# Rebuilding the main loop of a pairwise outer-product kernel with batch normalisation: larger tiles, two buffers, W in PSUM, products shared with GpSimd, and a fixed order

## The chip, the cores and the metric

The kernel runs on one core of a Trainium2 chip. The metric is the device time of one execution in microseconds (us). The engines are named as the profile names them: PE is TensorE, DVE VectorE, ACT ScalarE, POOL GpSimd, SP SyncE, which here only issues DMAs.

## The reference, cut to what matters

```python
# r_xi, r_xj: (1024, 39, 16) float32; W: (1, 16, 16); gamma, beta: (741,)
rows, cols = np.tril_indices(39, k=-1)                  # 741 pairs (r, c) with c < r
cross = xj[:, rows, :, None] * xi[:, cols, None, :]     # (1024, 741, 16, 16)
mean = jnp.mean(cross, axis=(0, 2, 3), keepdims=True)   # one mean and variance for each pair
var = jnp.mean(jnp.square(cross - mean), axis=(0, 2, 3), keepdims=True)
normed = (cross - mean) * jax.lax.rsqrt(var + 1e-5)
normed = normed * gamma[None, :, None, None] + beta[None, :, None, None]
out = normed[:, :, None, :, :] * W[None, None, :, :, :]  # stored as (1024, 1, 741, 16, 16)
```

The output has 1024 x 741 x 256 numbers of 4 bytes, 777 MB. It is nearly all that moves: the inputs have 6 MB.

## The kernel before

The 1024 samples lie on the 128 partitions, eight samples on each. A first part, the head, works out for each pair a scale `s` and a shift `t` (tiles `s_sb` and `t_sb`), so that an output is (xj[b, r, i] x xi[b, c, j] x s[r, c] + t[r, c]) x W[i, j]. The head ends with the instructions of lines 149 to 151, and it stays as it is.

Then comes the main loop. It goes over the rows r = 1 to 38, short and long ones in turn (1, 38, 2, 37, ...). Row r has r pairs, c = 0 to r - 1. A tile is one row of `nt` samples on each partition, with `nt` the largest of 1, 2, 4 and 8 for which nt x r is below 39; so rows 20 to 38 have one sample in a tile, rows 10 to 19 two, rows 5 to 9 four. Each tile takes four steps:

- GpSimd multiplies the row's r vectors of `xi` by their scales into `xs` (line 166). There are two buffers of `xs`.
- ScalarE makes the products with `xj`: for each sample and each i of 16 one instruction over r x 16 elements, with xj[b, r, i] as its scale (line 183), into the tile `y`. For rows up to 6 VectorE makes them instead, one instruction a sample (line 175). There are four buffers of `y`.
- VectorE does the last step in place: one `scalar_tensor_tensor` for each pair c over nt x 256 elements, (y + t) x W (line 191), with `y` and W both in SBUF.
- SyncE issues one DMA that stores the tile (line 199).

The scheduler of the tile framework orders the instructions on each engine, and an instruction waits on semaphores for what it reads and for the buffer that it writes.

Of the kernel before, what the change touches and what calls it, by code (L numbers as in the profile page):

```python
# [7 lines left out]
F32 = mybir.dt.float32  # L8
AF = mybir.ActivationFunctionType
ALU = mybir.AluOpType  # L10
AX = mybir.AxisListType

BN_EPS = 1e-5
# Rows of at most this many pairs have their outer products on VectorE, the longer ones on ScalarE.
VECTOR_ROW = 6


@with_exitstack
def tile_pair_outer_batchnorm(
# [18 lines left out]
    nc = tc.nc  # L38
    P = nc.NUM_PARTITIONS
    NB, F, E = xi.shape  # L40
    NT = NB // P
    EE = E * E
# [14 lines left out]
    out_v = out.rearrange("(p t) o n i j -> p t (o n i j)", t=NT)  # L57
# [6 lines left out]
    with tc.tile_pool(name="stat", bufs=1) as st, tc.tile_pool(  # L64
        name="dev", bufs=2
# [6 lines left out]
        ones = st.tile([P, P], F32, name="ones")  # L72
        nc.gpsimd.memset(ones, 1.0 / NB)
# [16 lines left out]
        ma, mb, va, vb = (x[:, :, :, 0] for x in (ma, mb, va, vb))  # L90
# [6 lines left out]
        def pairs(engine, rows, cols, name):  # L97
            q = st.tile([P, NT, NP], F32, name=name)
            for r in range(1, F):
                engine.tensor_tensor(  # L100
                    q[:, :, first[r] : first[r] + r],
                    rows[:, :, r : r + 1].to_broadcast([P, NT, r]),
                    cols[:, :, 0:r],
                    ALU.mult,
                )
            return q
# [20 lines left out]
        mean = st.tile([P, 1, NP], F32, name="mean")  # L127
# [4 lines left out]
            nc.scalar.activation(q_a[:, t], q_a[:, t], AF.Square)  # L132
        batch_mean(ps_v, [q_a], False, True)

        # rstd = 1 / sqrt(var + eps), with a Newton step behind the table's square root
        var = st.tile([P, NP], F32, name="var")
        for acc, (n0, n1) in zip(ps_v, halves):
            nc.vector.tensor_scalar_add(var[:, n0:n1], acc[:, : n1 - n0], BN_EPS)  # L138
# [2 lines left out]
        rstd = st.tile([P, NP], F32, name="rstd")  # L141
# [12 lines left out]
    order = []  # L154
    for k in range(1, (F - 1) // 2 + 1):
        order += [k, F - k]
    assert sorted(order) == list(range(1, F))

    rows = ctx.enter_context(tc.tile_pool(name="rows", bufs=4))
    scaled = ctx.enter_context(tc.tile_pool(name="scaled", bufs=2))  # L160
    for r in order:
        n0 = first[r]
        nt = max(n for n in (1, 2, 4, 8) if NT % n == 0 and (n == 1 or n * r < F))
        for t0 in range(0, NT, nt):
            xs = scaled.tile([P, nt, r, E], F32, tag="xs", name=f"xs_{r}_{t0}")
            nc.gpsimd.tensor_tensor(  # L166
                xs,
                xi_sb[:, t0 : t0 + nt, 0:r, :],
                s_sb[:, :, n0 : n0 + r, :].to_broadcast([P, nt, r, E]),
                ALU.mult,  # L170
            )
            y = rows.tile([P, nt, r, E, E], F32, tag="y", name=f"y_{r}_{t0}")
            for t in range(nt):
                if r <= VECTOR_ROW:
                    nc.vector.tensor_tensor(  # L175
                        y[:, t],
                        xs[:, t].unsqueeze(2).to_broadcast([P, r, E, E]),
                        xj_sb[:, t0 + t, r : r + 1, :].unsqueeze(3).to_broadcast([P, r, E, E]),
                        ALU.mult,
                    )  # L180
                else:
                    for i in range(E):
                        nc.scalar.activation(  # L183
                            y[:, t, :, i, :],
                            xs[:, t],
                            AF.Copy,
                            scale=xj_sb[:, t0 + t, r, i : i + 1],
                        )
            y2 = y.rearrange("p t n i j -> p t n (i j)")
            for c in range(r):  # L190
                nc.vector.scalar_tensor_tensor(  # L191
                    y2[:, :, c, :],
                    y2[:, :, c, :],
                    t_sb[:, n0 + c : n0 + c + 1],
                    w_sb.to_broadcast([P, nt, EE]),
                    ALU.add,
                    ALU.mult,
                )
            nc.sync.dma_start(
                out_v[:, t0 : t0 + nt, n0 * EE : (n0 + r) * EE],  # L200
                y.rearrange("p t n i j -> p t (n i j)"),
            )


# [26 lines left out]
```

## Time and profile before

| | before |
|---|---|
| median of 3 runs | 3103.07 us (3102.97 to 3104.05) |
| span of the profiled execution (first to last instruction) | 3100.0 us |
| outside the span, by the median | 3.07 us |
| VectorE busy | 2448.0 us (79%) |
| ScalarE busy | 2015.7 us (65%) |
| GpSimd busy | 1659.1 us (54%) |
| written to HBM | 776.99 MB |
| DMA queue of SyncE, share of 16 engines | 59.1% |

The profiled execution has no time of its own beside its span; its 3100.0 us and the median differ by 3.07 us, a tenth of a per cent, which lie before the first and behind the last instruction.

How to read the lines of the profile. A group of instructions is shown as line, engine, operation, `out<-in`, shapes (partitions x elements of one partition), `x` count, then busy us and mean ns of one, then idle us of the engine ahead of them and who ended most of it. "Busy" counts overlapping instructions once, so busy divided by count is the distance from one start to the next where a stream has no holes, and the mean, which holds the filling and draining of the pipeline too, is longer. A row of the waits has who waited for whom, the total, the number of times, the longest. A row of the chain or of the order of time has start, duration and instruction. A row of the DMA issues has the size and the median time from issue to landing.

### The profile page before, as it was taken

The page shows a single profiled execution, that of the slowest core. Times are in us where ns is not written, and L with a number is a line of the kernel's source. Part 1 is how long each engine was busy: PE and PEld are TensorE (multiplying, and loading weights), DVE is VectorE, ACT ScalarE, POOL GpSimd, SP SyncE. Part 2 cuts the span into 40 slices and gives each one's busy share as a digit, 9 for nine tenths or more (in the row PEclk, how much of TensorE's full clock was granted, in tenths as well). Part 3 has the DMA queues.
Part 4 walks back from the last instruction along what each step waited for, and adds up shares of the span by engine and source line. Part 5 has one row for each costly group of instructions (what it writes and reads, how often), then busy time and mean ns, then how long its engine had stood idle before and what let it go on. Part 6 is the DMA issues. An engine that isn't in the chain of part 4 may idle for free.

```text
span 3100.0 us, 10969 instructions
## 1 busy us (share of the span) xinstructions
PE 45.6 (1%) x128; PEld 26.7 (1%) x128; DVE 2448.0 (79%) x5253; ACT 2015.7 (65%) x4117; POOL 1659.1 (54%) x252
## 2 busy tenths in 40 slices
PE   2300000000000000000000000000000000000000
PEld 1100000000000000000000000000000000000000
DVE  8687888888888787777777787768777777778786
ACT  2446455464635777777676767676868686868685
POOL 2375757665666656555646464646363636362623
PEclk9655555555555555555555555555555555555555
DMA  2165656566555656666656656565656565666666
GB/s 78 78 265 228 282 244 259 250 269 271 250 252 248 293 237 281 256 268 268 288 249 263 265 240 272 246 281 242 270 243 281 244 281 249 276 263 268 275 267 275
DMA packets 43653, 783.71 MB, mean 253 GB/s; under 512 B 3472, under 2 KB 4496, under 8 KB 11824
## 3 DMA queue, kind: packets, MB, share of 16 engines
q1 hardware_dynamic: 42784, 779.56, 59.1%
q10 hardware_dynamic: 576, 2.56, 0.2%
q0 software_dynamic: 208, 0.89, 0.1%
q14 instruction: 84, 0.69, 0.1%
q8 instruction: 1, 0.02, 0.0%
HBM read 6.00 MB, written 776.99 MB: 253 GB/s over the span
## 4 chain that ended last, share of the span: by engine, by line
ACT 48%; POOL 45%; DVE 3%; issue 2%; PE 1%; DMA 0%; POOLq 0%; DVEq 0%; ACTq 0%
ACT y L183 48%; POOL xs L166 45%; PE ps_v L111 1%; DVE y L191 1%; DVE q_a L100 1%; DVE dev L86 0%; PE ps_m L111 0%; DMA xj_sb<-in_r_xj_dram 0%; DVE ma L83 0%; DVE vb L88 0%; DVE va L88 0%; DVE mb L83 0%; DVE inv L140 0%; DVE rstd L146 0%; DVE inv L144 0%
## 5 line engine op out<-in xcount | busy, mean ns | idle before, releaser
L191 DVE SCALAR_TENSOR_TENSOR y<-y,t_sb,w_sb 128x256 f32<-128x256 f32 (+2 forms) x5068 | 2314.6, 534 | 610.3 <-ACT y L183 610.1
L183 ACT ACTIVATE y<-xs,xj_sb 128x608 f32<-128x608 f32 (+31 forms) x4096 | 1994.9, 580 | 978.7 <-POOL xs L166 978.7
L166 POOL TENSOR_TENSOR xs<-xi_sb,s_sb 128x576 f32<-128x576 f32 (+19 forms) x206 | 1637.3, 7958 | 1368.8 <-ACT y L183 1315.6
L175 DVE TENSOR_TENSOR y<-xs,xj_sb 128x256 f32<-128x256 f32 (+5 forms) x48 | 51.5, 1136 | 1.5 <-POOL xs L166 1.4
L100 POOL TENSOR_TENSOR q_c<-va,sb 128x8 f32<-128x8 f32 (+37 forms) x38 | 19.6, 553 | 39.3 <-DVE sb L93 39.3
L87 ACT ACTIVATE dev<-dev 128x1248 f32<-128x1248 f32 x8 | 9.9, 1243 | 26.1 <-DVE dev L86 25.9
L129 ACT COPY mean<-ps_m 128x371 f32<-128x371 f32 (+1 forms) x2 | 0.9, 468 | 31.0 <-PE ps_m L111 31.0
L138 DVE TENSOR_SCALAR var<-ps_v 128x371 f32<-128x371 f32 (+1 forms) x2 | 1.1, 545 | 22.1 <-PE ps_v L111 22.0
L100 DVE TENSOR_TENSOR q_a<-ma,mb 128x8 f32<-128x8 f32 (+37 forms) x38 | 18.2, 554 | 0.0
L142 ACT ACTIVATE rstd<-inv 128x741 f32<-128x741 f32 x1 | 0.8, 822 | 25.9 <-DVE inv L140 25.9
L111 PE MATMUL ps_m<-q_a,ones 128*128 128x371 f32 (+1 forms) x32 | 15.7, 662 | 56.1 <-DVE q_a L100 56.1
L83 DVE TENSOR_REDUCE ma<-xj_sb 128x78 f32<-128x1248 f32 x4 | 5.8, 1452 | 6.9 <-DMA xj_sb<-in_r_xj_dram 6.9
L111 PE MATMUL ps_v<-q_a,ones 128*128 128x371 f32 (+1 forms) x32 | 10.2, 474 | 0.0
L111 PE MATMUL ps_v<-q_b,ones 128*128 128x371 f32 (+1 forms) x32 | 10.2, 474 | 0.0
L111 PE MATMUL ps_v<-q_c,ones 128*128 128x371 f32 (+1 forms) x32 | 10.1, 474 | 0.0
L100 DVE TENSOR_TENSOR q_b<-sa,vb 128x8 f32<-128x8 f32 (+37 forms) x38 | 9.9, 341 | 0.0
L111 PEld LDWEIGHTS ps_m<-q_a,ones 128*128 128x128 f32 x32 | 8.5, 274 | 62.7 <-issue 57.0
L131 DVE TENSOR_TENSOR q_a<-q_a,mean 128x741 f32<-128x741 f32 x8 | 6.8, 925 | 1.6 <-ACT mean L129 1.6
L132 ACT ACTIVATE q_a<-q_a 128x741 f32<-128x741 f32 x8 | 6.6, 822 | 1.1 <-DVE q_a L131 1.0
L111 PEld LDWEIGHTS ps_v<-q_a,ones 128*128 128x128 f32 x32 | 6.1, 189 | 3.9
L111 PEld LDWEIGHTS ps_v<-q_c,ones 128*128 128x128 f32 x32 | 6.1, 189 | 3.9
L111 PEld LDWEIGHTS ps_v<-q_b,ones 128*128 128x128 f32 x32 | 6.1, 189 | 3.9
(30 smaller groups left out, 49.6 us busy)
## 6 DMA issues: line engine op xcount, KB each, us to landing
out_dram<-y SPq DMA_DIRECT2D x14, 4608.0 KB, 12.4
out_dram<-y SPq DMA_DIRECT2D x15, 4096.0 KB, 11.2
out_dram<-y SPq DMA_DIRECT2D x12, 4864.0 KB, 12.9
out_dram<-y SPq DMA_DIRECT2D x12, 4352.0 KB, 11.8
out_dram<-y SPq DMA_DIRECT2D x14, 3584.0 KB, 10.0
out_dram<-y SPq DMA_DIRECT2D x15, 3072.0 KB, 8.8
out_dram<-y SPq DMA_DIRECT2D x12, 3840.0 KB, 10.6
out_dram<-y SPq DMA_DIRECT2D x12, 3328.0 KB, 9.3
```

The source lines that it names most:

```text
L83: nc.vector.tensor_reduce(ms[:, :, :, 0], xs, AX.X, ALU.add)
L87: nc.scalar.activation(dev, dev, AF.Square)
L100: engine.tensor_tensor(q[:, :, first[r] : first[r] + r], rows[:, :, r : r + 1].to_broadcast([P, NT, r]), cols[:, :, 0:r], ALU.mult,)
L111: nc.tensor.matmul(acc[:, : n1 - n0], ones, q[:, t, n0:n1], start=start and k == 0, stop=stop and k == len(qs) * NT - 1,)
L129: nc.scalar.copy(mean[:, 0, n0:n1], acc[:, : n1 - n0])
L131: nc.vector.tensor_sub(q_a[:, t], q_a[:, t], mean[:, 0])
L132: nc.scalar.activation(q_a[:, t], q_a[:, t], AF.Square)
L138: nc.vector.tensor_scalar_add(var[:, n0:n1], acc[:, : n1 - n0], BN_EPS)
L166: nc.gpsimd.tensor_tensor(xs, xi_sb[:, t0 : t0 + nt, 0:r, :], s_sb[:, :, n0 : n0 + r, :].to_broadcast([P, nt, r, E]), ALU.mult,)
L175: nc.vector.tensor_tensor(y[:, t], xs[:, t].unsqueeze(2).to_broadcast([P, r, E, E]), xj_sb[:, t0 + t, r : r + 1, :].unsqueeze(3).to_broadc ...
L183: nc.scalar.activation(y[:, t, :, i, :], xs[:, t], AF.Copy, scale=xj_sb[:, t0 + t, r, i : i + 1],)
L191: nc.vector.scalar_tensor_tensor(y2[:, :, c, :], y2[:, :, c, :], t_sb[:, n0 + c : n0 + c + 1], w_sb.to_broadcast([P, nt, EE]), ALU.add, AL ...
```

## The change

The main loop is written anew; the head is untouched.

- W is copied once into PSUM by ScalarE (`w_dve`, line 160). VectorE's last step reads it there. GpSimd reads W from SBUF as before.
- A tile has the largest `nt` of 1, 2, 4 and 8 with nt x r up to 76: two samples for rows 20 to 38, four for rows 10 to 19, eight for rows 1 to 9. There are 105 tiles, and two buffers of `y` where there were four; each buffer is twice as large.
- The rows go from 6 to 38 and then from 5 down to 1.
- Of the 16 products of a sample, 12 stay on ScalarE (line 204) and 4 go to GpSimd, as `tensor_scalar` (line 206). Rows up to 6 have them on VectorE as before (line 194).
- Of the pairs of a row above 6, 13% (rounded: 5 of 38, 4 of 30, 1 of 7) have their last step on GpSimd: one `tensor_scalar` for each pair that adds the shift (line 235), and one `tensor_tensor` for all of them that multiplies by W (line 239). VectorE has the others (line 219).
- The store of a tile is cut into pieces (line 229): after every 16/nt pairs of VectorE one DMA, and one for GpSimd's pairs at the end.
- The order on each engine is the order of the code: for each tile its last steps and stores, then the products of the next tile, then the `xs` of the one after that.

```diff
+    w_dve = wpsp.tile([P, 1, EE], F32, name="w_dve")          # a pool in PSUM
+    nc.scalar.copy(w_dve, w_sb)
+    def samples(r):
+        return max(n for n in (1, 2, 4, 8) if NT % n == 0 and (n == 1 or n * r <= UNITS))   # UNITS = 76
+    order = list(range(VECTOR_ROW, F)) + list(range(VECTOR_ROW - 1, 0, -1))                 # VECTOR_ROW = 6
+    tiles = [(r, t0, samples(r)) for r in order for t0 in range(0, NT, samples(r))]
-    rows = ctx.enter_context(tc.tile_pool(name="rows", bufs=4))
+    rows = ctx.enter_context(tc.tile_pool(name="rows", bufs=2))
     scaled = ctx.enter_context(tc.tile_pool(name="scaled", bufs=2))
+    def products(k):
...
+            for i in range(E):
+                scale = xj_sb[:, t0 + t, r, i : i + 1]
+                if i < E - POOL_I:                                                          # POOL_I = 4
+                    nc.scalar.activation(y[:, t, :, i, :], xs[:, t], AF.Copy, scale=scale)
+                else:
+                    nc.gpsimd.tensor_scalar(y[:, t, :, i, :], xs[:, t], scale, 1.0, ALU.mult, ALU.mult)
+    def finish(k):
...
+        split = r - (int(r * POOL_SHARE + 0.5) if r > VECTOR_ROW else 0)                    # POOL_SHARE = 0.13
+        step = max(1, 16 // nt)
...
+        for c in range(split, r):
+            nc.gpsimd.tensor_scalar(y[:, :, c, :], y[:, :, c, :], t_sb[:, n0 + c : n0 + c + 1], 1.0, ALU.add, ALU.mult)
+        if split < r:
+            nc.gpsimd.tensor_tensor(y[:, :, split:r, :], y[:, :, split:r, :],
+                w_sb.unsqueeze(1).to_broadcast([P, nt, r - split, EE]), ALU.mult)
+        for c0 in range(0, split, step):
+            c1 = min(c0 + step, split)
+            for c in range(c0, c1):
+                pair(c)          # VectorE: scalar_tensor_tensor(y, y, t, w_dve, add, mult)
+            store(c0, c1)        # SyncE: one DMA for these pairs
+        if split < r:
+            store(split, r)
+    with tc.manual_schedule():
+        scale_xi(0); products(0); scale_xi(1)
+        for k in range(len(tiles)):
+            finish(k)
+            if k + 1 < len(tiles): products(k + 1)
+            if k + 2 < len(tiles): scale_xi(k + 2)
```

The following rows show the order of the built programs around row 38. A name such as `y_38_2` is the tile of row 38 that begins with sample 2, the number behind it is that of the buffer's allocation, and the brackets hold the semaphores for which the instruction waits: an engine's name, or DMAHW0 to DMAHW7, on which the DMAs of SyncE and ScalarE report their landing in turn.

GpSimd at rows 38, 2 and 37 before: only `xs`, one for each tile.

```order
L166 TENSOR_TENSOR xs_38_6_740<-xi_sb_58,s_sb_61 128x608 [waits Activation_49,Pool_49]
L166 TENSOR_TENSOR xs_38_7_798<-xi_sb_58,s_sb_61 128x608 [waits Activation_49,Pool_49]
L166 TENSOR_TENSOR xs_2_0_856<-xi_sb_58,s_sb_61 128x256 [waits Activation_49,Pool_49]
L166 TENSOR_TENSOR xs_37_0_870<-xi_sb_58,s_sb_61 128x592 [waits Activation_49,Pool_49]
L166 TENSOR_TENSOR xs_37_1_927<-xi_sb_58,s_sb_61 128x592 [waits DVE_49,Pool_49]
```

GpSimd now, from the last step of one tile of row 38 to the `xs` after the next tile's products.

```order
L235 TENSOR_SCALAR y_38_0_7552<-y_38_0_7552,t_sb_62 128x2x256 [waits Activation_49,Pool_49]
L235 TENSOR_SCALAR y_38_0_7552<-y_38_0_7552,t_sb_62 128x2x256 x4
L239 TENSOR_TENSOR y_38_0_7552<-y_38_0_7552,w_sb_60 128x2x1280 [waits Pool_49]
L206 TENSOR_SCALAR y_38_2_7632<-xs_38_2_7585,xj_sb_59 128x38x16 [waits DMAHW5_49,DMAHW6_49,DMAHW4_49,DMAHW7_49,DMAHW0_49,DVE_49]
L206 TENSOR_SCALAR y_38_2_7632<-xs_38_2_7585,xj_sb_59 128x38x16 x7
L178 TENSOR_TENSOR xs_38_4_7665<-xi_sb_58,s_sb_61 128x1216
```

Between two `xs` there now stand five additions, a multiplication and eight products, and the first product waits for five DMAs.

ScalarE at row 38 before: 16 products for each sample, with a wait for one earlier store and for `xs`.

```order
L183 ACTIVATE y_38_2_510<-xs_38_2_508,xj_sb_59 128x38x16 [waits DMAHW3_49,Pool_49]
L183 ACTIVATE y_38_2_510<-xs_38_2_508,xj_sb_59 128x38x16 x15
L183 ACTIVATE y_38_3_568<-xs_38_3_566,xj_sb_59 128x38x16 [waits DMAHW0_49,DVE_49,Pool_49]
L183 ACTIVATE y_38_3_568<-xs_38_3_566,xj_sb_59 128x38x16 x15
L183 ACTIVATE y_38_4_626<-xs_38_4_624,xj_sb_59 128x38x16 [waits DMAHW1_49,DMAHW5_49,DVE_49,Pool_49]
```

ScalarE now: 24 products for two samples.

```order
L204 ACTIVATE y_38_2_7632<-xs_38_2_7585,xj_sb_59 128x38x16 [waits DMAHW4_49,DMAHW5_49,DMAHW0_49,DMAHW6_49,DVE_49,DMAHW7_49,Activation_49,Pool_49]
L204 ACTIVATE y_38_2_7632<-xs_38_2_7585,xj_sb_59 128x38x16 x23
L204 ACTIVATE y_38_4_7712<-xs_38_4_7665,xj_sb_59 128x38x16 [waits DMAHW3_49,DMAHW2_49,DMAHW4_49,DMAHW1_49,DMAHW5_49,DVE_49,DMAHW6_49,Activation_49,Pool_49]
L204 ACTIVATE y_38_4_7712<-xs_38_4_7665,xj_sb_59 128x38x16 x23
L204 ACTIVATE y_38_6_7792<-xs_38_6_7745,xj_sb_59 128x38x16 [waits DMAHW2_49,DMAHW1_49,DMAHW3_49,DMAHW0_49,DMAHW4_49,DVE_49,DMAHW7_49,Activation_49,Pool_49]
```

The first product of a tile waits for five or six DMAs: all stores of the tile two before, which lay in the same buffer.

SyncE before: one store of a whole tile, after VectorE's last instruction of it.

```order
L199 DMA out_0_dram<-y_38_3_568 128x9728 [waits DMAHW4_49,DVE_49,Activation_49]
L199 DMA out_0_dram<-y_38_4_626 128x9728 [waits DMAHW5_49,DVE_49,Activation_49]
L199 DMA out_0_dram<-y_38_5_684 128x9728 [waits DMAHW6_49,DVE_49,Activation_49]
L199 DMA out_0_dram<-y_38_6_742 128x9728 [waits DMAHW7_49,DVE_49,Activation_49]
L199 DMA out_0_dram<-y_38_7_800 128x9728 [waits DMAHW0_49,DVE_49,Activation_49]
```

SyncE now: the stores of one tile of row 38, and the first of the next.

```order
L229 DMA out_0_dram<-y_38_2_7632 128x2x2048 [waits DVE_49,DMAHW7_49,Activation_49,Pool_49]
L229 DMA out_0_dram<-y_38_2_7632 128x2x2048 [waits DMAHW0_49,DVE_49]
L229 DMA out_0_dram<-y_38_2_7632 128x2x2048 [waits DMAHW1_49,DVE_49]
L229 DMA out_0_dram<-y_38_2_7632 128x2x2048 [waits DMAHW2_49,DVE_49]
L229 DMA out_0_dram<-y_38_2_7632 128x2x256 [waits DMAHW3_49,DVE_49]
L229 DMA out_0_dram<-y_38_2_7632 128x2x1280 [waits DMAHW4_49,Pool_49]
L229 DMA out_0_dram<-y_38_4_7712 128x2x2048 [waits DVE_49,DMAHW5_49,Activation_49,Pool_49]
```

A tile of 38 pairs leaves in four stores of eight pairs, one of one pair and one of GpSimd's five; the store that waits for GpSimd stands behind VectorE's last one and ahead of the next tile's. Each store also waits for the DMA that used its DMAHW semaphore eight DMAs before.

More of the change, by code (lines that the diff above doesn't have):

```diff
@@ L15 @@
 VECTOR_ROW = 6
+UNITS = 76
+POOL_I = 4
+POOL_SHARE = 0.13
 @with_exitstack
@@ L151, in tile_pair_outer_batchnorm @@
         nc.vector.tensor_sub(t_sb, b_sb, t_sb)
[L154 to L157, printed above, removed]
-    rows = ctx.enter_context(tc.tile_pool(name="rows", bufs=4))
+    wpsp = ctx.enter_context(tc.tile_pool(name="wps", bufs=1, space=bass.MemoryType.PSUM))
+    w_dve = wpsp.tile([P, 1, EE], F32, name="w_dve")
+    nc.scalar.copy(w_dve, w_sb)
+    def samples(r):
+        return max(n for n in (1, 2, 4, 8) if NT % n == 0 and (n == 1 or n * r <= UNITS))
@@ L160, in tile_pair_outer_batchnorm, with scale_xi @@
+    order = list(range(VECTOR_ROW, F)) + list(range(VECTOR_ROW - 1, 0, -1))
+    tiles = [(r, t0, samples(r)) for r in order for t0 in range(0, NT, samples(r))]
+    rows = ctx.enter_context(tc.tile_pool(name="rows", bufs=2))
     scaled = ctx.enter_context(tc.tile_pool(name="scaled", bufs=2))
-    for r in order:
+    xs_of, y_of = {}, {}
+    def scale_xi(k):
+        r, t0, nt = tiles[k]
         n0 = first[r]
[L163 to L169, printed above, removed]
+        xs = scaled.tile([P, nt, r, E], F32, tag="xs", name=f"xs_{r}_{t0}")
+        nc.gpsimd.tensor_tensor(
+            xs,
+            xi_sb[:, t0 : t0 + nt, 0:r, :],
+            s_sb[:, :, n0 : n0 + r, :].to_broadcast([P, nt, r, E]),
+            ALU.mult,
+        )
+        xs_of[k] = xs
@@ new lines, in products @@
+    def products(k):
+        r, t0, nt = tiles[k]
+        xs = xs_of.pop(k)
+        y = rows.tile([P, nt, r, E, E], F32, tag="y", name=f"y_{r}_{t0}")
+        y_of[k] = y
+        for t in range(nt):
+            if r <= VECTOR_ROW:
+                nc.vector.tensor_tensor(
+                    y[:, t],
+                    xs[:, t].unsqueeze(2).to_broadcast([P, r, E, E]),
+                    xj_sb[:, t0 + t, r : r + 1, :].unsqueeze(3).to_broadcast([P, r, E, E]),
+                    ALU.mult,
+                )
+                continue
+            for i in range(E):
[3 more added lines that the diff above has]
+                else:
+                    nc.gpsimd.tensor_scalar(
+                        y[:, t, :, i, :], xs[:, t], scale, 1.0, ALU.mult, ALU.mult
+                    )
@@ L170, in tile_pair_outer_batchnorm, with pair @@
+    def finish(k):
+        r, t0, nt = tiles[k]
+        n0 = first[r]
+        y = y_of.pop(k).rearrange("p t n i j -> p t n (i j)")
+        split = r - (int(r * POOL_SHARE + 0.5) if r > VECTOR_ROW else 0)
+        step = max(1, 16 // nt)
+        def pair(c):
+            nc.vector.scalar_tensor_tensor(
+                y[:, :, c, :],
+                y[:, :, c, :],
+                t_sb[:, n0 + c : n0 + c + 1],
+                w_dve.to_broadcast([P, nt, EE]),
+                ALU.add,
                 ALU.mult,
@@ L171, in tile_pair_outer_batchnorm @@
             )
[L172 to L198, printed above, removed]
+        def store(c0, c1):
             nc.sync.dma_start(
-                out_v[:, t0 : t0 + nt, n0 * EE : (n0 + r) * EE],
-                y.rearrange("p t n i j -> p t (n i j)"),
-            )
+                out_v[:, t0 : t0 + nt, (n0 + c0) * EE : (n0 + c1) * EE],
+                y[:, :, c0:c1, :].rearrange("p t n e -> p t (n e)"),
+            )
@@ new lines, in finish @@
+        for c in range(split, r):
+            nc.gpsimd.tensor_scalar(
+                y[:, :, c, :], y[:, :, c, :], t_sb[:, n0 + c : n0 + c + 1], 1.0, ALU.add, ALU.mult
+            )
+        if split < r:
+            nc.gpsimd.tensor_tensor(
+                y[:, :, split:r, :],
+                y[:, :, split:r, :],
+                w_sb.unsqueeze(1).to_broadcast([P, nt, r - split, EE]),
+                ALU.mult,
+            )
+        for c0 in range(0, split, step):
[3 more added lines that the diff above has]
+            store(c0, c1)
@@ L206 @@
+        if split < r:
+            store(split, r)
+    with tc.manual_schedule():
+        scale_xi(0)
+        products(0)
+        scale_xi(1)
+        for k in range(len(tiles)):
+            finish(k)
+            if k + 1 < len(tiles):
+                products(k + 1)
+            if k + 2 < len(tiles):
+                scale_xi(k + 2)
 _INS = ["r_xi", "r_xj", "L0_rec_W", "L0_rec_gamma", "L0_rec_beta"]
```

## The prediction, made before the changed kernel was run

> I read the page first (busy shares, the chain that ended last, the costliest groups), then the waits, then the chain and the order of time around one long row, then single groups, some of them cut to a short window, for prices.
>
> **What bounds the kernel now.** No engine is busy all the time: VectorE, the busiest, works 79% of the span, and the chain that ended last alternates between ScalarE and GpSimd. Below stand the page's first lines, its chain by engine, and two rows of the waits (total, times, longest).
>
> ```profile
> span 3100.0 us, 10969 instructions
> PE 45.6 (1%) x128; PEld 26.7 (1%) x128; DVE 2448.0 (79%) x5253; ACT 2015.7 (65%) x4117; POOL 1659.1 (54%) x252
> ACT 48%; POOL 45%; DVE 3%; issue 2%; PE 1%; DMA 0%; POOLq 0%; DVEq 0%; ACTq 0%
> POOL xs L166 <- ACT y L183: 1315.6, 148, 17.5
> ACT y L183 <- POOL xs L166: 978.7, 56, 28.9
> ```
>
> The two wait for each other: GpSimd 1315.6 us for a free `xs`, ScalarE 978.7 us for a filled one. Why GpSimd takes so long shows where row 38 is worked: two single `xs` instructions of the same shape (groups in a short window; the last columns are busy us, mean ns, idle before), what VectorE ran over the second one (order of time: start, us), and the chain there (start, us).
>
> ```profile
> L166 POOL TENSOR_TENSOR xs<-xi_sb,s_sb 128x608 f32<-128x608 f32 x1 | 1.2, 1221 | 0.0
> L166 POOL TENSOR_TENSOR xs<-xi_sb,s_sb 128x608 f32<-128x608 f32 x1 | 36.1, 36075 | 9.6 <-ACT y L183 9.6
> 196.56 34.91 DVE L191 SCALAR_TENSOR_TENSOR y<-y,t_sb,w_sb 128x256 f32<-128x256 f32 x88
> 196.48 36.08 POOL xs L166
> 235.53 0.54 issue
> 236.06 10.54 ACT y L183 x16
> 254.99 25.21 POOL xs L166
> ```
>
> The same 608 elements take 1.22 us alone and 36.1 us while 88 last steps stream through VectorE: GpSimd does not share, it is shut out until the stream has a hole. ScalarE then lacks its `xs`, VectorE drains and idles, and GpSimd gets in. From 196.48 to 254.99, 58.5 us, the chain makes two samples of row 38.
>
> **The change, part by part.** (1) W comes from PSUM, so that a last step reads one tensor from SBUF instead of two, and I take it that GpSimd is then not shut out. No row of before has a VectorE instruction with one SBUF input beside a GpSimd one, so this is a choice, and the chance that it is wrong stands among the rivals. Where it holds, the 36 us stall goes, the `xs` of a two-sample tile (1216 elements) takes 0.18 + 1216 x 0.001715 = 2.3 us by the price of (4), and what is late next is the landing of stores (6). The Trainium skill, SBUF — State Buffer, section Who interferes with whom, says that a VectorE instruction with two SBUF inputs contends with a GpSimd instruction that reads SBUF, and that one with at most one SBUF input, outside the 2-port modes, does not. The 36.1 us agree with its first half; for the second half no row speaks.
>
> (2) VectorE's price. Steps back to back, and a PSUM source beside an SBUF one:
>
> ```profile
> L191 DVE SCALAR_TENSOR_TENSOR y<-y,t_sb,w_sb 128x512 f32<-128x512 f32 x12 | 8.0, 740 | 0.0
> 760.55 6.06 DVE L191 SCALAR_TENSOR_TENSOR y<-y,t_sb,w_sb 128x1024 f32<-128x1024 f32 x5
> L138 DVE TENSOR_SCALAR var<-ps_v 128x370 f32<-128x370 f32 x1 | 0.5, 546 | 0.1
> L145 DVE TENSOR_SCALAR inv<-inv 128x741 f32<-128x741 f32 x1 | 0.5, 549 | 0.0
> L175 DVE TENSOR_TENSOR y<-xs,xj_sb 128x1536 f32<-128x1536 f32 x8 | 14.5, 1859 | 0.7 <-POOL xs L166 0.7
> L175 DVE TENSOR_TENSOR y<-xs,xj_sb 128x256 f32<-128x256 f32 (+5 forms) x48 | 51.5, 1136 | 1.5 <-POOL xs L166 1.4
> ```
>
> A step costs 8.0/12 = 0.667 us at 512 elements and 6.06/5 = 1.212 at 1024, hence 1.06 ns an element and, by two more such increments, 2.30 us at 2048. The PSUM source (370 elements, 546 ns) is no dearer than the SBUF one (741 in 549 at two elements a cycle), so I add nothing for PSUM; as the far end I keep +10% of a 512 step, 0.065 us. The Trainium skill, VectorE: DVE Perf Modes, section on the TRN2 errata, gives 58 cycles of fixed cost from SBUF and 120 from PSUM, 65 ns more at 0.96 GHz; by it VectorE would have 2187 x 0.065 = 142 us more and the sum below would end at 2346 us. The rows of L138 and L145 speak against that, but not for an instruction with two tensors.
>
> In rows above 6 the tiles are 76 of two samples, 20 of four, 3 of eight; VectorE keeps 1912, 254 and 21 steps: 1912 x 0.667 + 254 x 1.212 + 21 x 2.30 = 1631 us = D. Larger tiles save fixed cost (2187 steps for 5036), and 752 of all 5928 pair-samples go to GpSimd.
>
> (3) ScalarE loses 4 of 16 products:
>
> ```profile
> L183 ACT ACTIVATE y<-xs,xj_sb 128x608 f32<-128x608 f32 (+31 forms) x4096 | 1994.9, 580 | 978.7 <-POOL xs L166 978.7
> L183 ACT ACTIVATE y<-xs,xj_sb 128x608 f32<-128x608 f32 x128 | 88.9, 789 | 57.9 <-POOL xs L166 57.9
> ```
>
> The shapes stay, so A = 1994.9 x 12/16 = 1496 us (at row 38, 88.9/128 = 0.695 us each).
>
> (4) GpSimd gains 1024 products (368,640 elements a partition), 331 additions (192,512), 99 multiplications by W (192,512), beside `xs` (94,848 in 105 instructions).
>
> ```profile
> L166 POOL TENSOR_TENSOR xs<-xi_sb,s_sb 128x320 f32<-128x320 f32 x1 | 0.7, 727 | 0.0
> L73 POOL MEMSET ones<- 128x128 f32 x1 | 0.2, 223 | 0.0
> L217 POOL MEMSET const-float32-0.0<- 128x1 f32 x1 | 0.1, 98 | 0.2 <-issue 0.2
> ```
>
> Two inputs: (1221 - 727)/288 = 1.715 ns an element and 0.178 us fixed, so 287,360 elements and 204 instructions take 529 us. One tensor input has no row; it lies between a memset, (223 - 98)/127 = 0.98 ns and 0.097 us, and the two-input price: 561,152 elements in 1355 instructions take 681 to 1203 us. GpSimd's sum is 1210 to 1732 us, I take the middle, 1471. Either end stays under the loop's length below, and inside a tile too: at row 38 and the upper end its last step (9.8 us) and products (9.7) fill 19.5 of 24 us. So it costs nothing while it runs beside the others; without that cover see the rivals.
>
> (5) Stores. 206 become 466 on SP's one queue, in pieces of 16 pair-samples, GpSimd's share last.
>
> ```profile
> out_dram<-y SPq DMA_DIRECT2D x14, 2560.0 KB, 7.6
> out_dram<-y SPq DMA_DIRECT2D x12, 4864.0 KB, 12.9
> out_dram<-y SPq DMA_DIRECT2D x1, 4096.0 KB, 11.1
> out_dram<-y SPq DMA_DIRECT2D x2, 4096.0 KB, 11.4
> out_dram<-y SPq DMA_DIRECT2D x1, 4096.0 KB, 12.0
> out_dram<-y SPq DMA_DIRECT2D x1, 2048.0 KB, 7.5
> HBM read 6.00 MB, written 776.99 MB: 253 GB/s over the span
> ```
>
> 2304 KB more take 5.3 us: 445 GB/s, with 1.7 us that don't depend on size. The three stores of 4096 KB are of rows 32, 8 and 4 with 32, 8 and 4 KB in one run: 11.1, 11.4, 12.0, so beyond the 1.7 us 8 KB runs (two samples) cost 3% more and 4 KB runs (four) 10%; 2 KB runs (row 2: 5.8 us for 4.7) 23%. All bytes take 776.99/0.445 = 1746 us, with these shares, of 74, 20 and 6% of the bytes, about 1845. Each store also waits for the eighth before it, which has landed by then (a tile has 4 to 6), and GpSimd's share, last on the queue and ahead of the next tile's stores, is done some 10 us after the products at row 38, before VectorE's 22.
>
> (6) The new wait. The `y` buffers go from 4 to 2, and ScalarE's first product of a tile waits for every store of the tile two before. Behind it stand all its products, and so VectorE's next tile. A buffer goes round: products (A), last steps (D), time T until its last store has landed; two buffers, so a tile needs half a round. T by the pieces left when VectorE ends, 0.61 us a pair of two samples: row 38 leaves 8, 1 and 5 pairs, 14 x 0.61 + 1.7 less the last step, 0.7: 9.5 us; row 29 (8, 1, 4) 8.9; row 24 (5 and 3, with 1.5 us of a piece of 8) 8.1. Mean 8.8, x 76 = 669 us; four samples about 10 (1.29 us a pair; the queue falls behind a little) x 20 = 200; eight about 13 x 3 = 39. T = 908 us. Row 38: (16.7 + 22.0 + 9.5)/2 = 24.1 us for two samples, against 58.5 now; its stores alone need 23.2.
>
> (7) Semaphores: the 0.54 us ahead of ScalarE, with 0.16 at the two other hand-overs, is 0.7 a round, 0.35 x 99 = 35 us.
>
> **The sum.** Loop: (1496 + 1631 + 908)/2 + 35 = 2053 us. Before it:
>
> ```profile
> 111.50 0.94 DVE s_sb L149
> L142 ACT ACTIVATE rstd<-inv 128x741 f32<-128x741 f32 x1 | 0.8, 822 | 25.9 <-DVE inv L140 25.9
> out_dram<-y SPq DMA_DIRECT2D x1, 1024.0 KB, 4.8
> ```
>
> The copy of W to PSUM, 256 elements, falls into ScalarE's 25.9 idle us ahead of the root and costs nothing. `s` is ready at 112.4 as now, VectorE free two such steps later, at 114.5; row 6 on VectorE takes 14.5 of products and 6 x 2.30 of last steps, until 143. After it rows 5 to 1 on VectorE alone: 51.5 - 14.5 = 37 of products, 15 x 2.30 = 34.5, a last store 4.8: 76. 143 + 2053 + 76 = 2272, and with the 3.07 us by which the median of the runs (3103.07) exceeds the profiled span, **2275 us**. Without the change the same parts are the span itself, so the change is worth -828 us.
>
> Its own range: T with no penalty and no queue (830), 0.2 us a round: 2210; below that, 2130, if some waits of the round overlap. Above: PSUM +65 ns, half of 142 us: +71; 1.7 us that two pieces behind one another don't hide, +3.4/2 x 99 = +170, not both whole: 2450.
>
> **The rivals.** *GpSimd still shut out* (the other side; the change then doesn't do what it says). If a last step with W in PSUM locks GpSimd out as now, GpSimd's sum doesn't lie beside VectorE's but behind it: 143 + 1631 + (1210 to 1732) + 76 + 3 = 3063 to 3585, at the middle 3324 us, slower. It decides once GpSimd's work exceeds VectorE's idle 422 us in the loop. For it: the 36.1 us. Against it: all of these were two SBUF reads. 0.08.
>
> *GpSimd the bound.* Above (2053 - 529 - 241)/561,152 = 2.29 ns an element for one-input work GpSimd is longer than the loop; at 2.5 ns its 2173 us give 143 + 2173 + 76 + 3 = 2395 us, at 3 ns 2675. For it: writes in runs of 16 elements, which no row prices. Against: two inputs cost 1.715. 0.14.
>
> *The round doesn't bind.* If refilling overlaps more than the whole-tile wait allows, the stores bind: first piece at 114.5 + 14.5 + 4.6 = 134, + 1845 + 5 + 3 = 1987 us. For it: row 38's 23.2 against 24.1. Against: the wait names all stores of a tile. 0.08.
>
> **Chances.** The round-trip case has 0.70. A difference over 0.2% is about what can be told from none here. Faster: 0.70 + 0.14 + 0.08 and 0.01 of the lock's low end, 0.93; same 0.01; slower 0.06. The range, 2130 to 2450, holds nearly all of 0.70 and half or more of GpSimd's 0.14, and leaves out both outer rivals.
>
> **What would show it.** GpSimd's `xs` of 1216 elements at 0.18 + 2.09 = 2.3 us beside VectorE (2.3 right, tens of us: lock); last steps of 512 at 0.67 apart (0.73: PSUM costs); ScalarE's wait at L204 put down to landing stores, about 9 us from VectorE's last step of a tile to the last landing; GpSimd's one-input price between 0.98 and 1.72 ns; the DMA share of the whole span up from 0.59 to about 0.85. The prediction is wrong if GpSimd is the releaser of VectorE's L219 in most tiles, or ScalarE starts a tile before the stores of the tile two before have landed.

## The result, and the profile after

The changed kernel takes 2282.64 us (median of 4 runs, 2280.94 to 2283.89) beside 3103.19 us before: ratio 0.7355, 95% interval 0.7345 to 0.7366, about 820 us less. The forecast was 2275 us, range 2130 to 2450. The profiled execution took 2280.94 us and has a span of 2279.2.

The page's first lines and the groups that the sum rests on (busy us, mean ns of one, then idle us ahead of the group and who ended most of it):

```profile
span 2279.2 us, 9501 instructions
PE 44.7 (2%) x128; PEld 25.9 (1%) x128; DVE 1799.0 (79%) x2393; ACT 1523.5 (67%) x3094; POOL 1435.2 (63%) x1605
L219 DVE SCALAR_TENSOR_TENSOR y<-y,t_sb,w_dve 128x512 f32<-128x512 f32 x1912 | 1265.6, 743 | 261.7 <-issue 248.9 <-ACT y L204 12.8
L204 ACT ACTIVATE y<-xs,xj_sb 128x112 f32<-128x112 f32 (+31 forms) x3072 | 1502.3, 581 | 571.9 <-DMA out_dram<-y 387.9
L206 POOL TENSOR_SCALAR y<-xs,xj_sb 128x112 f32<-128x112 f32 (+31 forms) x1024 | 567.6, 577 | 47.2 <-DMA out_dram<-y 46.7
L235 POOL TENSOR_SCALAR y<-y,t_sb 128x512 f32<-128x512 f32 (+2 forms) x331 | 242.3, 750 | 612.9 <-ACT y L204 612.9
L239 POOL TENSOR_TENSOR y<-y,w_sb 128x2048 f32<-128x2048 f32 (+3 forms) x99 | 425.5, 4298 | 8.2
L178 POOL TENSOR_TENSOR xs<-xi_sb,s_sb 128x1216 f32<-128x1216 f32 x6 | 13.6, 2271 | 0.0
```

VectorE is still 79% busy, now of a shorter span. An `xs` of 1216 elements takes 2.27 us, where half as many took up to 36 us before, so the lock is gone. A last step with W in PSUM takes 1265.6/1912 = 0.662 us, no longer than with W in SBUF. What is left is a wait for stores. The waits (total, times, longest), row 38 in order of time (start, us, and the idle time ahead in brackets), the chain there, and the queue:

```profile
POOL y L235 <- ACT y L204: 612.9, 99, 15.0
DVE y L219 <- issue: 410.8, 94, 24.4
ACT y L204 <- DMA out_dram<-y: 387.9, 61, 16.5
2108.11 21.82 DVE L219 SCALAR_TENSOR_TENSOR y<-y,t_sb,w_dve 128x512 f32<-128x512 f32 x33 [2.71 <-issue]
2115.29 16.73 ACT L204 ACTIVATE y<-xs,xj_sb 128x608 f32<-128x608 f32 x24 [7.26 <-issue]
2132.11 18.52 DVE L219 SCALAR_TENSOR_TENSOR y<-y,t_sb,w_dve 128x512 f32<-128x512 f32 x28 [2.18 <-issue]
2139.84 10.49 ACT L204 ACTIVATE y<-xs,xj_sb 128x608 f32<-128x608 f32 x15 [7.82 <-DMA out_dram<-y]
2123.35 6.59 DVE y L219 x10
2130.42 9.31 DMA out_dram<-y
2139.84 7.50 ACT y L204 x11
q1 hardware_dynamic: 170848, 779.58, 85.2%
```

The chain now goes round a buffer. VectorE ends a tile at 2129.9, its last piece is issued at 2130.42 and lands 9.3 us after that, ScalarE starts at 2139.84, and VectorE starts 2132.11 - 2108.11 = 24.0 us after the tile before: the 24.1 of the prediction. "issue" stands where the profile has no releaser. By the times, VectorE starts a tile within 0.21 us of ScalarE's last product in 97 of the 99 tiles above row 6, while GpSimd's last product was done at least 3.1 us before in all of them.

### The profile page after: what moved, and what is told of

Same layout as the page of the kernel before. It is cut to its first block, busy times and chain, and to the rows that moved or that the text cites. A ratio compares the mean times of both kernels' runs of the same rounds, so it can differ in the third digit from the quotient of the medians.

```text
span 2279.2 us, 9501 instructions
## 1 busy us (share of the span) xinstructions
PE 44.7 (2%) x128; PEld 25.9 (1%) x128; DVE 1799.0 (79%) x2393; ACT 1523.5 (67%) x3094; POOL 1435.2 (63%) x1605
## 3 DMA queue, kind: packets, MB, share of 16 engines
q1 hardware_dynamic: 170848, 779.58, 85.2%
HBM read 6.00 MB, written 776.99 MB: 344 GB/s over the span
## 5 line engine op out<-in xcount | busy, mean ns | idle before, releaser
L219 DVE SCALAR_TENSOR_TENSOR y<-y,t_sb,w_dve 128x512 f32<-128x512 f32 (+2 forms) x2208 | 1665.4, 835 | 442.5 <-issue 410.8
L204 ACT ACTIVATE y<-xs,xj_sb 128x112 f32<-128x112 f32 (+31 forms) x3072 | 1502.3, 581 | 571.9 <-DMA out_dram<-y 387.9
L235 POOL TENSOR_SCALAR y<-y,t_sb 128x512 f32<-128x512 f32 (+2 forms) x331 | 242.3, 750 | 612.9 <-ACT y L204 612.9
L206 POOL TENSOR_SCALAR y<-xs,xj_sb 128x112 f32<-128x112 f32 (+31 forms) x1024 | 567.6, 577 | 47.2 <-DMA out_dram<-y 46.7
L239 POOL TENSOR_TENSOR y<-y,w_sb 128x2048 f32<-128x2048 f32 (+3 forms) x99 | 425.5, 4298 | 8.2
L178 POOL TENSOR_TENSOR xs<-xi_sb,s_sb 128x768 f32<-128x768 f32 (+20 forms) x105 | 183.2, 1745 | 107.2 <-DVE y L194 58.2
L194 DVE TENSOR_TENSOR y<-xs,xj_sb 128x1536 f32<-128x1536 f32 (+5 forms) x48 | 50.2, 1119 | 0.1
```

Source lines behind the costliest of these rows:

```text
L178: nc.gpsimd.tensor_tensor(xs, xi_sb[:, t0 : t0 + nt, 0:r, :], s_sb[:, :, n0 : n0 + r, :].to_broadcast([P, nt, r, E]), ALU.mult,)
L194: nc.vector.tensor_tensor(y[:, t], xs[:, t].unsqueeze(2).to_broadcast([P, r, E, E]), xj_sb[:, t0 + t, r : r + 1, :].unsqueeze(3).to_broadc ...
L204: nc.scalar.activation(y[:, t, :, i, :], xs[:, t], AF.Copy, scale=scale)
L206: nc.gpsimd.tensor_scalar(y[:, t, :, i, :], xs[:, t], scale, 1.0, ALU.mult, ALU.mult)
L219: nc.vector.scalar_tensor_tensor(y[:, :, c, :], y[:, :, c, :], t_sb[:, n0 + c : n0 + c + 1], w_dve.to_broadcast([P, nt, EE]), ALU.add, ALU ...
L235: nc.gpsimd.tensor_scalar(y[:, :, c, :], y[:, :, c, :], t_sb[:, n0 + c : n0 + c + 1], 1.0, ALU.add, ALU.mult)
```

## The experiments

All ran on the same kind of input as before, each against runs of the kernel before on its own chip; ratios are to that kernel.

The theory: W in PSUM ends the exclusion of GpSimd, and then the round of two `y` buffers, half of products (A), last steps (D) and landing (T), sets the time. Rivals: GpSimd's lock was not the matter; the stores' bandwidth, not the round, is the bound.

**1. W read from SBUF again.**

```diff
-                w_dve.to_broadcast([P, nt, EE]),
+                w_sb.to_broadcast([P, nt, EE]),
```

> Undoes one part: VectorE's last step reads W from SBUF again, all else as changed. Shut-out theory: GpSimd gets in only when VectorE's stream has a hole, so GpSimd's 1419 us in the loop lie behind VectorE's 1618 instead of beside: 144 + 1618 + 1419 + 76 = about 3260 us, anything from 3000 to 3350; single GpSimd instructions of tens of us. Rival, that W's place does not matter and larger tiles and sharing made it fast: 2283 us within 15.

Measured: 2954.29 us (2953.26 to 2956.02), ratio 0.9527 [0.9513, 0.9541]: 672 us slower than the change, and below the 3000 to 3350 expected for the lock. The page's engines, two groups, and a stretch of row 38 in order of time:

```profile
PE 45.3 (2%) x128; PEld 26.3 (1%) x128; DVE 2722.7 (92%) x2393; ACT 1523.8 (52%) x3094; POOL 2299.1 (78%) x1605
L219 DVE SCALAR_TENSOR_TENSOR y<-y,t_sb,w_sb 128x512 f32<-128x512 f32 x1912 | 1983.4, 1113 | 97.0 <-POOL y L206 80.5 <-issue 16.5
L206 POOL TENSOR_SCALAR y<-xs,xj_sb 128x608 f32<-128x608 f32 x32 | 53.8, 1699 | 35.0 <-DMA out_dram<-y 35.0
2697.49 5.88 POOL L239 TENSOR_TENSOR y<-y,w_sb 128x2560 f32<-128x2560 f32 x1
2697.86 33.88 DVE L219 SCALAR_TENSOR_TENSOR y<-y,t_sb,w_sb 128x512 f32<-128x512 f32 x43
2720.51 17.11 POOL L206 TENSOR_SCALAR y<-xs,xj_sb 128x608 f32<-128x608 f32 x8 [17.14 <-DMA out_dram<-y]
2737.59 2.26 POOL L178 TENSOR_TENSOR xs<-xi_sb,s_sb 128x1216 f32<-128x1216 f32 x1
2737.66 22.48 DVE L219 SCALAR_TENSOR_TENSOR y<-y,t_sb,w_sb 128x512 f32<-128x512 f32 x14 [5.91 <-POOL y L206]
2739.84 5.52 POOL L235 TENSOR_SCALAR y<-y,t_sb 128x512 f32<-128x512 f32 x5
2745.44 5.91 POOL L239 TENSOR_TENSOR y<-y,w_sb 128x2560 f32<-128x2560 f32 x1
```

Here each keeps the other out, in turn. The 43 steps take 33.88 us, 5.4 more than 43 x 0.662, which is GpSimd's multiplication at their start. Eight products, 6.2 us of work at 0.775 each in the changed kernel, end 5.9 us after VectorE's stream. Then 14 steps take 22.48 instead of 9.3 us beside 13.7 us of GpSimd's work, in which `xs` and the multiplication run near their own speed (2.26 and 5.91 us, in the changed kernel 2.27 and 5.60) and the five additions do not (5.52 for 3.36). So the conflict is real and goes both ways; it lengthens VectorE's steps from 743 to 1113 ns in the mean and is not the complete serial order that the prediction's rival priced (3324). By the times of the changed kernel, the loop holds 1618 us of VectorE's and 1412 us of GpSimd's own work, and it took 2736 here: some 290 us overlap. A tile of row 38 takes 37.7 us where the two in turn would take 39.0, one of row 24 22.3 for 25.4. What decides who gets in was not settled.

**2. The kernel before with W in PSUM, and nothing else.**

```diff
+    w_dve = wpsp.tile([P, 1, EE], F32, name="w_dve")
+    nc.scalar.copy(w_dve, w_sb)
-                    w_sb.to_broadcast([P, nt, EE]),
+                    w_dve.to_broadcast([P, nt, EE]),
```

> The kernel before with one part of the change alone: W in PSUM for VectorE's last step. Shut-out theory: xs takes 1.2 us each, ScalarE no longer waits for it, VectorE (2236 us of last steps, 51 of products) and in the rows below 20 ScalarE bound the loop: 2410 us (VectorE alone) to 2570 (the longer of the two in each row), most of the change's gain by itself. Rival, that the larger tiles, the sharing and the order are what counts: about 3100.

Measured: 2413.32 us (2413.13 to 2413.85), ratio 0.7783 [0.7772, 0.7795].

```profile
PE 44.7 (2%) x128; PEld 25.9 (1%) x128; DVE 2347.9 (97%) x5253; ACT 2017.2 (84%) x4118; POOL 226.5 (9%) x252
```

The same 252 GpSimd instructions fall from 1659.1 us to 226.5, and VectorE becomes the bound at 97%. This one part is worth 687 us by itself, beside the 3100.5 of the kernel before on the same chip, and 672 when taken out of the change; all the rest is worth some 150 (experiment 1) to 130 (this one). So about five sixths of the gain is the place of W. The Trainium skill, SBUF — State Buffer, section Who interferes with whom, names the VectorE instruction with two inputs in SBUF as the one that conflicts with a GpSimd instruction that reads SBUF, and the one with at most one, outside the 2-port modes, as free of it; the two runs agree with both halves.

**3 and 4. ScalarE's share of the products**, all 16 of 16, and 10 of 16:

```diff
-POOL_I = 4
+POOL_I = 0        # experiment 3
+POOL_I = 6        # experiment 4
```

> Undoes one part: all 16 products of a sample on ScalarE, none on GpSimd. Round-trip theory (half of products + last steps + landing): ScalarE's 1502 us become 2003, the loop (2003 + 1618 + 972)/2 + 14 = 2310, the time about 2530 us. Rival, that the stores' bandwidth is the bound (DMA busy 96% from 1400 to 2200 us): unchanged at 2283, since ScalarE's 2003 + 144 is below it. Rival, that GpSimd is the bound: faster, it loses 568 us.

> Moves more of the same: 10 products on ScalarE, 6 on GpSimd. Round trip: ScalarE 1252 us, the loop (1252 + 1618 + 972)/2 + 14 = 1935, the time about 2155; up to 2220 if the landing time T grows because the stores come closer together. Rival, bandwidth: 2283 unchanged. Rival, GpSimd as a bound: its 1419 + 284 = 1703 us stay under the loop, so slower than 2283 only if its waits add up.

Measured: 2530.16 us (2529.13 to 2530.49), ratio 0.8158 [0.8146, 0.8171], and 2168.73 us (2167.86 to 2169.72), ratio 0.6995 [0.6983, 0.7006]. ScalarE's groups:

```profile
L204 ACT ACTIVATE y<-xs,xj_sb 128x112 f32<-128x112 f32 (+31 forms) x4096 | 1997.4, 580 | 325.7 <-DMA out_dram<-y 207.3
L204 ACT ACTIVATE y<-xs,xj_sb 128x112 f32<-128x112 f32 (+31 forms) x2560 | 1254.0, 581 | 707.3 <-DMA out_dram<-y 459.2
```

ScalarE gets 495 us more work in the one and 248 less in the other, and the time moves by +247.5 and -113.9, half of the one and 46% of the other: two buffers, half a round. In the second, T (the time from VectorE's last step of a tile to its last landing) grew, from 972 us over the 99 tiles to 1001. A kernel bound by VectorE, by GpSimd or by the stores would not have moved so. The second also beats the change, since GpSimd had room.

**5. Stores that wait for nothing.** They read `xj_sb` instead of `y`, in the same pieces, so that no buffer waits for a landing.

```diff
-                y[:, :, c0:c1, :].rearrange("p t n e -> p t (n e)"),
+                xj_sb.rearrange("p t f e -> p (t f e)")[:, : nt * (c1 - c0) * EE].rearrange("p (t e) -> p t e", t=nt),
```

> The changed kernel with its stores of the same sizes and places in the output, but read from the input tile xj instead of y, so they wait for no engine and no buffer of y waits for a landing; the output holds no results. Round trip without T: (1502 + 1618)/2 is below VectorE's own 1618, so the engines end at about 144 + 1618 + 76 = 1840 us; the stores alone, from the start at 417 GB/s or a little less for the short runs, at 1865 to 1920. Time 1850 to 1920. Rival, the stores' bandwidth is what the 2283 us are: the time stays above 2150. Rival, the engines are: last step of VectorE still near 2280.

Measured: 1931.33 us (1930.99 to 1931.46), ratio 0.6229 [0.6219, 0.6238], a little over the range.

```profile
HBM read 6.00 MB, written 776.99 MB: 406 GB/s over the span
PE 44.6 (2%) x128; PEld 26.0 (1%) x128; DVE 1792.5 (93%) x2393; ACT 1521.9 (79%) x3094; POOL 1435.8 (74%) x1605
q1 hardware_dynamic: 170848, 779.58, 100.6%
```

The stores start at 19 us and keep the queue full to the end, so this run shows what they alone take: 776.99 MB at 406 GB/s, 1914 us. The change issues its first store at 134.9 us, so by its stores alone it would end at about 2052, some 230 below what it takes; over the whole loop the wait, not the bandwidth, is its bound. The two come closer as the rows grow: a tile of row 24 takes 17.5 us in the change where its stores alone take 15.3 here, one of row 37 takes 23.9 where they take 23.4.

The engines ended later than expected, VectorE's last step at 1917 us and not at about 1840. The expectation compared sums over the loop, but in rows up to 19 a tile's products on ScalarE take longer than its last steps on VectorE (row 12: 16.7 beside 12.0 us, and here a tile every 16.9).

**6. Four buffers of half the size.**

```diff
-UNITS = 76
+UNITS = 38
-    rows = ctx.enter_context(tc.tile_pool(name="rows", bufs=2))
+    rows = ctx.enter_context(tc.tile_pool(name="rows", bufs=4))
```

> Undoes the tile size and the number of buffers together: one sample for rows 20 to 38, two for rows 10 to 19, four buffers of y of half the size; the memory is the same. Round trip: with four buffers a quarter of a round, no longer a bound; VectorE is, with more and shorter last steps (3824 x 0.396 + 508 x 0.662 + 42 x 1.196 = 1900 us for 1618): 144 + 1900 + 90 = about 2135 us, faster than the change, VectorE without holes. Rival, larger tiles save time: VectorE's 282 us more are added, 2565, or half of them, 2424. Rival, bandwidth: 2230 to 2283, by longer runs in the stores.

Measured: 2170.52 us (2170.03 to 2170.77), ratio 0.6999 [0.6989, 0.7010]. The engines, and two stretches of the loop (stretch, length, then busy us of PE, PEld, DVE, ACT and POOL, clock, DMA share, GB/s):

```profile
PE 44.4 (2%) x128; PEld 26.1 (1%) x128; DVE 2066.8 (95%) x4591; ACT 1530.0 (71%) x3094; POOL 1538.1 (71%) x2136
150.00:700.00 550.00, 0.00 (x0) 0.00 (x0) 486.87 (x815) 518.67 (x1363) 454.35 (x702) 0.50 0.98 393
700.00:2095.00 1395.00, 0.00 (x0) 0.00 (x0) 1395.00 (x3558) 964.03 (x1619) 1038.84 (x1346) 0.50 0.93 386
```

With four buffers the round is off the path at an equal size of memory, and the small tiles' price shows: 4591 VectorE instructions, and from 700 us on VectorE is busy without a hole, as expected. Up to 700 us the queue is the fuller one, at 98%, and VectorE is not; the time is 36 us above the 2135 expected.

**7 and 8. A taper of the pieces**, to shorten T: the first piece a quarter as large, the last ones halved, GpSimd's store in the middle; the second with `POOL_I = 6` too.

```diff
-        for c0 in range(0, split, step):
-            c1 = min(c0 + step, split)
+        while c0 < split:
+            left = split - c0
+            n = max(1, step // 4) if c0 == 0 else step if left > step + step // 2 else max(1, (left + 1) // 2)
...
+            if not pool_stored and 2 * c0 >= split:
+                store(split, r)
```

> The changed kernel with the stores cut otherwise: a first piece of a quarter, halving pieces at the end, GpSimd's store in the middle. Same work, same bytes, more and shorter runs. Round trip: less is left when VectorE ends, T falls from about 9.8 to about 5 us a tile, the loop by half of that: (1502 + 1618 + 480)/2 = 1800, then the stores at 417 GB/s (1863 us) bind the long rows: about 2100 us, 2070 to 2150. Rival, T does not count (bandwidth is the bound already): 2283, or more by the shorter runs.

> Both, the stores of e7 and 6 products on GpSimd. Round trip (1254 + 1618 + 480)/2 = 1676 is below the stores' 1863, so those bind: 134 + 1863 + 20 to 60, 2020 to 2060 us. If the round still binds: below e7 by 100 or more. If GpSimd (1695 us) binds through its waits: near e3's 2169.

Measured: 2293.11 us (2292.48 to 2293.77), ratio 0.7396 [0.7384, 0.7407], and 2192.44 us (2191.82 to 2193.08), ratio 0.7071 [0.7059, 0.7083]. Both expectations missed: each is slower than the same kernel without the taper, by 10 and 24 us. T, added up over the 99 tiles above row 6, is 987 us where it was 972. The small pieces landed no sooner than the large ones (in the first of the two 9.1 us after their issue for 256 KB, 6.7 for 2048 KB), which led to the next two.

**9 and 10. Half of the bytes**, without the taper and with it.

```diff
         def store(c0, c1):
+            c1 = c0 + (c1 - c0 + 1) // 2
```

> The changed kernel, each store cut to the first half of its pairs (rounded up), so that 52% of the output is written; every instruction and every wait stays. If T, the time from VectorE's last step to the last landing, is mostly the bytes that the queue still holds from before, the queue is empty in each tile now, and T is only the last pieces: at row 38 the 4 + 1 + 3 pairs left, 8 x 0.61 + 1.7 - 0.7 = 5.9 us, at row 24 4.7, some 550 over the 99 tiles instead of 972; loop (1502 + 1618 + 550)/2 + 14 = 1849, time about 2070. If T is a latency that does not depend on the bytes, T stays near 972 and the time near 2280.

> The tapered pieces (small first piece, halving last pieces, GpSimd's store in the middle) with each store cut to the first half of its pairs, 58% of the output. With all bytes the taper gained nothing (2293 beside 2283). If that was because the queue had not emptied, it gains now: T is the last one or two pairs, about 2.6 us a tile, 257 in all; loop (1502 + 1618 + 257)/2 + 14 = 1703, time 1925 (not under VectorE's 1800 busy and head), some 145 us under the run with half the bytes and whole pieces. If small stores cost as much in waiting as they save, it is again no faster than that run, about 2070.

Measured: 1995.54 us (1995.11 to 1996.41), ratio 0.6436 [0.6426, 0.6445], and 1971.06 us (1970.55 to 1972.56), ratio 0.6356 [0.6345, 0.6367]. DMA issues (count, KB each, median us to landing) of the taper with all bytes, then of the taper with half of them:

```profile
out_dram<-y SPq DMA_DIRECT2D x180, 512.0 KB, 7.7
out_dram<-y SPq DMA_DIRECT2D x120, 256.0 KB, 9.1
```

```profile
out_dram<-y SPq DMA_DIRECT2D x214, 512.0 KB, 3.3
out_dram<-y SPq DMA_DIRECT2D x244, 256.0 KB, 2.2
```

A piece of 256 KB lands after 9.1 us where the queue still holds earlier pieces, and after 2.2 where it doesn't. T over the 99 tiles falls from 972 to 355 with half the bytes, where 550 were expected, and with the taper to 270, near the 257 expected; a latency that doesn't depend on the bytes is out. So with all bytes T is mostly backlog, bytes that the queue still holds when VectorE ends, and this taper did not shorten it. The taper gains 24 us once the backlog is gone, not 145, and both times miss what was expected, the first by 75 us below, the second by 46 above: T was shorter than expected without the taper already, and VectorE comes next. In 43 of the 99 tiles of the tapered run its own steps are longer than half a round (row 38: 21.8 for 20.4). With the longer of the two for each tile, the loops add up to 2046, 1749 and 1727 us (change, half, half with taper), for 2060, 1775 and 1751 measured.

**11 and 12. What the runs point to:** four buffers of one-sample tiles, with GpSimd's share moved from products to last steps; the second run is the same kernel again.

```diff
-POOL_I = 4
-POOL_SHARE = 0.13
+POOL_I = 3
+POOL_SHARE = 0.19        # beside UNITS = 38 and bufs=4
```

> The four buffers of one-sample tiles of the earlier run (2170.5 us, VectorE 2066.8 us busy), with GpSimd's share of the last steps raised from 13% to 19% and its share of the products cut from 4 to 3 of 16. By the groups of that run VectorE's last steps fall from 1935 to about 1935 x 0.81/0.87 = 1801 us, so VectorE to some 1930; GpSimd goes to about 1700 to 1770, ScalarE to 1655. If VectorE was what set 2170, the time falls to 2030 to 2110, where the stores are the bound (148 us of head, 777 MB at 406 GB/s and a short tail, about 2070). If the stores already set it there, it stays within 20 us of 2170.

> One more look at the same kernel as the first of these runs, for its profile: 2030 to 2110 us.

Measured: 2097.13 us (2096.84 to 2097.88), ratio 0.6763 [0.6753, 0.6774], and 2096.87 us. The first run's engines, and the busy tenths of its DMA engines and what they moved in 40 slices of the span:

```profile
PE 44.7 (2%) x128; PEld 26.3 (1%) x128; DVE 1939.3 (93%) x4295; ACT 1654.5 (79%) x3350; POOL 1730.1 (83%) x2176
DMA  3047888999999999999999999999999999999986
GB/s 115 0 173 284 340 329 354 375 393 405 414 414 422 417 421 412 416 418 417 418 412 408 413 419 422 416 415 414 409 411 407 408 419 418 414 413 409 412 338 243
```

This beats both kernels, the change by 185.5 us, 8%. The stores now run at 405 to 422 GB/s from the tenth slice to the 38th, so more than small things would need fewer bytes or an earlier start of the stores.

## Why the prediction was right

The time was right to 7.6 us, by these steps and with these errors. The times of the tiles come from the trace: sums over the 99 tiles of rows above 6.

| term | predicted | measured in the change |
|---|---|---|
| A, ScalarE's products | 1496 | 1502.5 |
| D, VectorE's last steps | 1631 | 1617.7 |
| T, landing of the stores | 908 | 971.8 |
| hand-overs (measured: what is left of the loop) | 35 | 13.8 |
| loop | 2053 | 2059.8 |
| head and row 6 | 143 | 143.6 |
| rows 5 to 1 | 76 | 75.8 |

- *W in PSUM.* Taken on a choice, and right: experiments 1 and 2. The rival's price was too high, 3324 with a low end of 3063 where taking the part back measured 2954. It set GpSimd's work wholly behind VectorE's, and in part the two overlap. So even with W in SBUF the rest of the change is faster than before, by some 150 us, where the rival had it slower.
- *VectorE's price.* 0.667 us forecast, 0.662 measured; the 0.065 us held as a far end did not show. The Trainium skill's VectorE: DVE Perf Modes, section on the TRN2 errata, by which the sum ended at 2346, is not borne out for an instruction with one tensor from each memory.
- *ScalarE.* Right, and experiments 3 and 4 show its weight in the sum: one half.
- *GpSimd.* One-input work, L206 and L235, took 567.6 + 242.3 = 810 us, within 681 to 1203. The multiplications by W were priced too cheap: 425.5 us, where 1.715 ns an element and 0.178 us for each of the 99 give 348. GpSimd's four groups in the loop, 1419 us, came out near the middle, 1471, by opposite errors, which is luck. None of it is on the path: VectorE's wait ends with ScalarE's last product. The prediction's check at row 38 left out the tile's `xs`, 2.3 us, beside its 19.5 of 24; the four measured there are 17.2.
- *T.* Mis-sized: 64 us too short, half of it in the time. The mean of a two-sample tile is 9.3 us and not 8.8, of four 11.0 and not 10. The prediction counted the pieces left when VectorE ends (9.5 us at row 38, where the mean is 10.0) and gave the queue falling behind only "a little". The count came near, but it is not what sets T: by it the taper would have halved T, which stayed at 987 (experiment 7), and half of the bytes would have left 550, where 355 were measured (experiment 9). What the two show to set it is the backlog of the queue, which is 85% busy over the span and 96% from 1400 to 2200 us.
- *Stores.* 1845 us forecast by the size of single stores; all of them together take 1914 (experiment 5), 4% more. The rival in which they bind, 1987, would have been nearer 2052.
- *Hand-overs.* 0.14 us a tile and not 0.35; this error and that of D (13 us, half of it in the time) cancel most of T's. So the mechanism held, but that only 7.6 us are left is luck.
- *What would show it.* All the marks but one came as named: `xs` 2.3 us (2.27), steps 0.67 (0.662), ScalarE's wait put down to stores (387.9 of 571.9 us), about 9 us to the last landing (9.3 for two samples), the DMA share 0.85 (85.2%). The one that did not is GpSimd's one-input price, which, taken between the shapes of 608 and 320 elements, is below its lower end of 0.98: (775 - 535)/288 = 0.83 ns, with 0.27 us fixed, above the dearer end's 0.178.

```profile
L206 POOL TENSOR_SCALAR y<-xs,xj_sb 128x608 f32<-128x608 f32 x32 | 24.0, 775 | 0.0
L206 POOL TENSOR_SCALAR y<-xs,xj_sb 128x320 f32<-128x320 f32 x32 | 16.3, 535 | 11.6 <-DMA out_dram<-y 11.6
```

Where the expected gain of the other parts went: after W in PSUM VectorE is the bound at 2413 us, and the larger tiles and GpSimd's share take it from 2348 busy us to 1799. Only 131 of these 549 us reach the time, because two large buffers make each tile wait for its stores. Four small ones with the shares moved bring 316.

## What to carry to other kernels

Before dividing work anew, look for an engine whose single instructions take many times their price beside another engine's stream; moving one operand to PSUM was worth five sixths of this whole rewrite. Where a buffer is filled, finished and stored in turn, add up one round and divide it by the number of buffers, and take the longer of that and the busiest engine for each tile. Before cutting stores into smaller last pieces, look at how full the queue is: here they shortened T only with half of the bytes (355 to 270 us); with all bytes and the queue 85% busy they did not (972 to 987), and four buffers of half the size did what they could not.

## What the runs showed of the hardware that was not expected

- The exclusion goes both ways: in experiment 1, 14 VectorE steps took 22.48 us instead of 9.3 beside 13.7 us of GpSimd's work, which by itself takes 11.2.
- A multiplication by W on GpSimd costs (5599 - 3431)/1024 = 2.12 ns an element, where `xs`, also with two tensors, costs 1.715. `xs` uses each scale for 16 elements in a row, and W changes with each element; that this is the cause was not tried. The Trainium skill, GPSIMD Engine Reference, section on elementwise accounting, has 4497 ns for an addition of two tensors of 2048 elements, and the trace agrees with 4518 for a multiplication: the prediction would have been nearer with it than with the `xs` rows.

```profile
L239 POOL TENSOR_TENSOR y<-y,w_sb 128x2560 f32<-128x2560 f32 x16 | 89.6, 5599 | 1.3
L239 POOL TENSOR_TENSOR y<-y,w_sb 128x2048 f32<-128x2048 f32 x51 | 230.4, 4518 | 4.2
L239 POOL TENSOR_TENSOR y<-y,w_sb 128x1536 f32<-128x1536 f32 x28 | 96.1, 3431 | 2.3
```

- One GpSimd instruction over one tensor is cheaper by element than a memset of before seemed to be (0.83 beside 0.98 ns).
